# Attention probabilities turned through VectorE and DRAM instead of TensorE, in a two-layer graph attention kernel

## The chip, the cores and the metric

The kernel runs on one core of one Trainium2 chip, in fp32 throughout. The metric is device time in microseconds for one execution. A profiled execution gives the traces that are read below.

## The reference

The input x has 128 groups of 64 nodes with 768 features, and adj is a 64 x 64 mask per group. Two residual graph layers follow each other. Layer 0, which the change touches, has 12 heads of 64 features:

```python
h = jnp.einsum('bnd,ade->bane', feat_in, W)
th = jnp.tanh(h)
attn = th @ w_src + swapaxes(th @ w_dst)          # per head, 64 x 64
attn = jnp.where(attn >= 0, attn, 0.2 * attn)
attn = jnp.where(~adj, -999.0, attn)
attn = jax.nn.softmax(attn, axis=-1)
feat_out = elu(jnp.einsum('banm,bame->bane', attn, h) + b)
gate = jax.nn.sigmoid(feat_in @ H_w.T + H_b)
return gate * feat_out + (1.0 - gate) * feat_in
```

x plus this result is normalised over its features. Layer 1 is an attention with 6 heads of 128 features over the same groups of 64, masked by adj, with products by Wq, Wk, Wv and Wf, and again a sum with x and a normalisation. The change leaves it as it is; only the values of layer 1 (product by Wv) are made while layer 0 runs.

## The kernel before

Rows of x (group and node) are cut into 64 tiles of 128 rows, two groups to a tile, and two tiles make a pair: 32 pairs. Layer 0 takes the first half of the run, one pair after another. For each pair p there are fifteen "a" products (a scheme that saves multiplications, over the 768 x 1536 matrix of W and H_w; class `Fifteen`, L944) and seven "v" products (`Job`, L345) that make the values of layer 1 for earlier pairs. The table `TURN` writes out by hand in which order these 22 products of a pair follow each other on TensorE; "u" is a v product of pair p - 2, "v" one of pair p - 1. `EARLY` and `LAST` do the same for the first four pairs and the end.

Everything else of layer 0 is hung onto these products. The tables `NEW`, `OLD` and `SUMS` (with variants for early and last pairs) hold a due time for each small step, in units of products. `NEW` counts from the products that the step needs, `OLD` from the begin of the pair that follows the step's own pair. The loop over `items` (at the end of layer 0) issues one product, then all steps due at that place, in order of their due times. Each engine runs its instructions strictly in the order of issue. All transfers of layer 0 are issued by the SP queue, in order too: when one transfer has to wait, those behind it wait with it. Three buffers matter below: `pT` (one), `work` tiles (five) and the PSUM banks "m" (two).

For a tile t the steps around the change are these:

- `products` (L984 to L986) takes the tanh of h and multiplies it by the two weight rows; `terms` (L994 to L999) sums per head and turns the sums by a VectorE stream transpose, which turns each block of 32 x 32 by itself; `send` (L1003) stores them in DRAM and `fetch` (L1008) loads them back, broadcast to all rows of their group, as `dd`.
- `logits` and `more_logits` (L1037, ScalarE, 12 instructions) add the two terms with the leaky slope; `masked` (L1051, L1057, VectorE) puts in the mask and takes the row maxima.
- `exps` (L1066, ScalarE, 12 instructions) takes the exponentials into `prob`: rows are nodes n, columns are (head, node m).
- `probs_by_nodes` (L1081) turns `prob` so that m is on the partitions: six TensorE transposes of 128 x 128 into PSUM and two ScalarE copies into `pT`, both in the helper `transposed` (L1078, L1079). The same helper turns x1 later, in `by_features`.
- `other_half` (L1024, L1025) loads `hx`, the half of h that lies on the other group's partitions.
- `attend` (L1099) multiplies: for each of six columns j, two halves of the heads a and two groups g, a matmul with a 64 x 64 block of `pT` as its weights and 65 columns of h or `hx` as its moving operand (the 65th is ones and gives the denominator of the softmax). That makes 24 matmuls per tile.
- `features` (L1115, L1116, L1123) and `elu1`, `gated`, `stats`, `power`, `normed`, `by_features`, `spill_rows` go on to the tile's normalised rows, and `v_begins` starts the sums for the v products.

For the odd tile of a pair (`probs1`, `attend1`) the place of attention is behind the sixth product of the next pair's `TURN`, for the even one (`probs0`, `attend0`) behind the eleventh.

Of the kernel before, what the change touches and what calls it, by code (L numbers as in the profile page):

```python
# [9 lines left out]
F32 = mybir.dt.float32  # L10
# [5 lines left out]
P = 128  # L16
N = 64
# [4 lines left out]
HALF = D // 2  # L22
H0, E0 = 12, 64
J0 = H0 // 2
# [106 lines left out]
]  # L131
TURN = "u6 a1 u5 a0 u7 a5 a3 u3 a8 u4 a6 a7 a9 a10 a2 a12 a4 a14 a11 v1 a13 v2".split()

EARLY = (
    "a0 a5 a3 a8 a6 a1 a7 a10 a9 a2 a12 a4 a11 a14 a13".split(),
# [9 lines left out]
SUMS = dict(next6=0.2, next9=0.4, next2=4.5, next3=6.2, next0=7.2, next5=10, next8=5.3, own10=3.7, own12=7.2,  # L145
    own13=2.7)
OLD = dict(probs1=3.8, gtanh1=0, resid1=3.6, attend1=5.3, feat1=5.5, elu1=7.2, gated1=7.4, stats1=7.5, pow1=9,
    norm1=10.1, byf1=11.3, spill1=13.9, logits0=2.3, leaky0=3.1, masked0=4, exps0=5, gtanh0=5.6,
    resid0=7.2, probs0=8, attend0=10.5, feat0=10.8, elu0=12.5, gated0=12.6, stats0=15, pow0=15.2,
    norm0=16.1, byf0=17.2, spill0=22.3, sum0=15.6, sum1=18, sum2=22, sum3=27, spillT=22, spillV=12.8,  # L150
    mask=8.9, adj=4.5, xT=1.4, inputs1=10.3, inputs0=17.5, plus1=16.3, plus0=19.2)
NEW_LAST = dict(tanh1=2, terms1=4, bias1=6.4, send1=4.7, hx1=10.9, fetch1=9.3, logits1=9.6, leaky1=10.4,
    masked1=11, exps1=12.5, tanh0=1.8, terms0=5, bias0=5, send0=6.2, hx0=4.9, fetch0=8.3, gbias0=10.8,
    gbias1=2.2)
SUMS_LAST = dict(next6=0.4, next9=6.4, next2=0.6, next3=5, next0=15.7, next5=0.1, next8=11.3, own10=1.2, own12=7.8,
    own13=10.6)
OLD_LAST = dict(probs1=2.1, gtanh1=0.8, resid1=5.8, attend1=5, feat1=5.5, elu1=7, gated1=7.4, stats1=9.3,
    pow1=10.8, norm1=11.6, byf1=13.3, spill1=14.5, logits0=3, leaky0=3.4, masked0=4.4, exps0=5,
    gtanh0=8, resid0=9.7, probs0=8.8, attend0=10.5, feat0=11.8, elu0=12.4, gated0=12.8, stats0=14.5,
    pow0=14.6, norm0=15.6, byf0=16.5, spill0=22.4, sum0=16.5, sum1=17.2, sum2=18.5, sum3=24.4,  # L160
    spillT=24.8, spillV=11, mask=5.1, adj=-1.3, xT=3.4, inputs1=5.9, inputs0=18.5, plus1=13.6,
    plus0=18.9)
OLD_EARLY = [
    dict(probs1=1.8, gtanh1=-2, resid1=0, attend1=3.5, feat1=5, elu1=6, gated1=6.1, stats1=7, pow1=8,
        norm1=9, byf1=10, spill1=12.3, logits0=3.5, leaky0=4.3, masked0=5.2, exps0=6.2, gtanh0=3.5,
        resid0=4.8, probs0=8.3, attend0=11, feat0=12, elu0=12.2, gated0=13.1, stats0=14.5, pow0=15,
        norm0=15.2, byf0=17.5, spill0=18, sum0=10.2, sum1=18, sum2=19.3, sum3=26.7, spillT=18.4,
        spillV=11.2, mask=6, adj=3.7, xT=0, inputs1=10.2, inputs0=17.3, plus1=12.2, plus0=18.8),
    dict(probs1=-4.1, gtanh1=1.3, resid1=2.5, attend1=3, feat1=4.7, elu1=5.1, gated1=5.8, stats1=6.8,
        pow1=7, norm1=8, byf1=10.3, spill1=10.7, logits0=3, leaky0=4, masked0=5, exps0=6.3, gtanh0=2.7,  # L170
        resid0=6.8, probs0=8.3, attend0=9.7, feat0=10.5, elu0=12, gated0=12.4, stats0=13, pow0=14,
        norm0=16, byf0=17, spill0=21.7, sum0=11.7, sum1=18, sum2=19.5, sum3=24.7, spillT=22.2,
        spillV=15.2, mask=9, adj=5.2, xT=-3.5, inputs1=8.2, inputs0=11.7, plus1=17, plus0=15.2),
    dict(probs1=1, gtanh1=1.6, resid1=4.3, attend1=3.5, feat1=4, elu1=4.2, gated1=5.4, stats1=7.7,
        pow1=8.5, norm1=10.5, byf1=11.3, spill1=13.2, logits0=2.8, leaky0=3.8, masked0=5, exps0=7.3,
        gtanh0=-1.3, resid0=6.6, probs0=8.3, attend0=9.5, feat0=11.5, elu0=12, gated0=12.1, stats0=13.3,
        pow0=13.5, norm0=14, byf0=16.3, spill0=18, sum0=16.5, sum1=18.2, sum2=16, sum3=21, spillT=16.8,
        spillV=8, mask=5, adj=-4.8, xT=2.9, inputs1=10.2, inputs0=13.5, plus1=11.7, plus0=17),
    dict(probs1=1.8, gtanh1=1.3, resid1=1.8, attend1=3.5, feat1=4.5, elu1=6, gated1=6.4, stats1=7.4,
        pow1=8, norm1=9, byf1=11.5, spill1=14.8, logits0=2.7, leaky0=4.3, masked0=4.5, exps0=5.9,  # L180
        gtanh0=-0.8, resid0=7.7, probs0=8, attend0=9, feat0=10.5, elu0=11.2, gated0=12.1, stats0=14,
        pow0=15, norm0=16, byf0=17.2, spill0=18.3, sum0=14.8, sum1=18.5, sum2=22, sum3=20, spillT=21.1,
        spillV=11.6, mask=8.7, adj=2, xT=-0.2, inputs1=13.5, inputs0=16, plus1=13.6, plus0=19.7),
]
# [27 lines left out]
def kernel(  # L212
# [611 lines left out]
    with ExitStack() as ph, ExitStack() as ph_r:  # L824
# [69 lines left out]
        def work(name):  # L894
            return sb.tile([P, D], F32, tag="work", name=name, bufs=5)
# [164 lines left out]
        def exps(t):  # L1060

            att, mx = st[t].pop("att"), st[t].pop("mx")
            prob = work(f"prob_{t}")
            for a in range(H0):
                at = 2 * (a % J0) + a // J0
                S.activation(  # L1066
                    prob[:, at * N : (at + 1) * N],
                    att[:, a * N : (a + 1) * N],
                    AF.Exp,
                    bias=mx[:, a : a + 1],  # L1070
                )
            st[t]["prob"] = prob

        def transposed(dst, src, name):

            b = bank("m", name)
            for c in range(3):
                T.transpose(b[:, c * P : (c + 1) * P], src[:, c * P : (c + 1) * P], ident)  # L1078
# [12 lines left out]

        def attend(t):
            pT, h, hx = st[t].pop("pT"), h_of(t), st[t].pop("hx")
            av = [bank("m", f"av_{t}_{a}") for a in range(2)]
            for j in range(J0):
                for a in range(2):
                    rows = slice(a * N, (a + 1) * N)
                    for g in range(2):
                        T.matmul(  # L1099
                            av[a][g * N : (g + 1) * N, j * EP : (j + 1) * EP],  # L1100
                            pT[rows, j, g * N : (g + 1) * N],
                            h[rows, a * J0 + j, :] if a == g else hx[rows, j, :],
                            start=True,
                            stop=True,
                        )
            st[t]["av"] = av
# [154 lines left out]
        for p in range(NP + 1):  # L1261
# [15 lines left out]

            if q >= 0:
                for key, f in (
                    ("probs", probs_by_nodes), ("gtanh", gate_tanh), ("resid", residual), ("attend", attend),  # L1280
                    ("feat", features), ("elu", elu1), ("gated", gated), ("stats", stats), ("pow", power),
                    ("norm", normed), ("byf", by_features), ("spill", spill_rows),
                ):
# [246 lines left out]
```

## Time and profile before

| | |
|---|---|
| median of the runs | 2811.52 us (2810.82 to 2812.22, 2 runs) |
| the profiled execution's own time | 2813.49 us |
| its span, from the first to the last instruction | 2811.7 us |
| mean granted TensorE clock | 0.997 |
| TensorE busy / VectorE / ScalarE / GpSimd | 99% / 66% / 48% / 52% of the span |
| layer 0 | about the first 1450 us |
| one pair of layer 0 (644.0 to 688.4 us) | TensorE 44.4 us busy, VectorE 33.4, ScalarE 30.3, GpSimd 26.6 |
| transposes of prob (L1078, pTp) | 384, mean 276 ns, 55.4 us busy |
| their copies (L1079, pT) | 128, median 478 ns |
| attention matmuls (L1099, av) | 3072 instructions on TensorE, two for each matmul |
| DMA | 198038 packets, 325.52 MB |

The profile names engines PE (TensorE matmuls), PEld (TensorE weight loads), DVE (VectorE), ACT (ScalarE), POOL (GpSimd) and SP. A line of a group or of a timeline gives the source line, engine, operation, what is written <- what is read, and shapes. Times in a timeline count from the start of the span. A line of stretches gives, for each engine, its busy time with the number of instructions in brackets, then the granted TensorE clock, the DMA share and the GB/s. Matmuls are pipelined: the duration of one is longer than its distance to the next, so the work of TensorE is read from start to start. The rows of transfers give the number, the size of each and the median time from issue to landing.

### The profile page before, as it was taken

How to read it: one execution, taken by the hardware profiler on the slowest of the kernel's cores; microseconds unless marked ns; L12 is line 12 of the kernel's file. 1: busy time of each engine (PE TensorE's matmuls, PEld its weight loads, DVE VectorE, ACT ScalarE, POOL GpSimd, SP SyncE). 2: the span in 40 equal slices, each digit the busy share in tenths (PEclk: the TensorE clock that was granted, in tenths of full speed). 3: DMA queues.
4: the chain of work that ended last, by engine and by line, in shares of the span. 5: the costliest groups of instructions: out<-in, count | busy, mean ns of one | idle time of the engine just before them, and what ended most of it. 6: DMA issues, size and time to landing. Idle time of an engine off the chain costs nothing.

```text
span 2811.7 us, 47352 instructions
## 1 busy us (share of the span) xinstructions
PE 2776.4 (99%) x17472; PEld 1931.9 (69%) x17472; DVE 1851.2 (66%) x3215; ACT 1357.1 (48%) x3434; POOL 1453.7 (52%) x1501
## 2 busy tenths in 40 slices
PE   7999999999999999999999999999999999999998
PEld 3455555555555555555568888888888888888887
DVE  7867877777777777867764555555555555554557
ACT  4666676766767666676753222333222333221333
POOL 5556556565655656555454345445345435345435
PEclk9999999999999999999999999999999999999999
DMA  5354444544545445333444112222212222212212
GB/s 186 110 167 155 137 159 133 173 151 143 167 138 165 147 148 166 110 125 104 170 163 161 63 52 88 91 83 80 69 48 86 91 84 80 72 50 81 91 61 83
DMA packets 198038, 325.52 MB, mean 116 GB/s; under 512 B 46896, under 2 KB 125744, under 8 KB 197808
## 3 DMA queue, kind: packets, MB, share of 16 engines
q1 hardware_dynamic: 197520, 322.10, 34.8%
q8 instruction: 139, 2.28, 0.3%
q14 instruction: 91, 0.75, 0.1%
q10 hardware_dynamic: 288, 0.39, 0.0%
HBM read 198.48 MB, written 111.15 MB: 110 GB/s over the span
## 4 chain that ended last, share of the span: by engine, by line
PE 95%; DVE 1%; ACT 0%; issue 0%; DMA 0%; POOL 0%; ACTq 0%; DVEq 0%
PE y_a L944 18%; PE z_a L944 9%; PE z_q L524 9%; PE z_k L524 9%; PE y_v L345 9%; PE z_o L571 9%; PE y_k L524 6%; PE y_q L524 6%; PE y_o L571 6%; PE z_v L345 4%; PE x_v L345 2%; PE av L1099 2%; PE cp L689 2%; PE sp L629 2%; PE pTp L1078 2%; PE x1Tp L1078 1%
## 5 line engine op out<-in xcount | busy, mean ns | idle before, releaser
L944 PE MATMUL y_a<-wa,sx 128*128 128x512 f32 x1024 | 487.3, 605 | 19.2 <-DVE sx L882 7.9
L944 PEld LDWEIGHTS y_a<-wa,sx 128*128 128x128 f32 x1024 | 189.3, 192 | 221.6 <-issue 173.4
L488 POOL TENSOR_TENSOR so<-ctxT 128x256 f32<-128x256 f32 x224 | 157.7, 728 | 287.8 <-ACT ctxT L716 286.9
L716 ACT ACTIVATE ctxT<-cp,bv_c 128x256 f32<-128x256 f32 x192 | 73.8, 486 | 451.1 <-PE cp L689 451.1
L1129 POOL TENSOR_TENSOR x<-hg,x 128x768 f32<-128x768 f32 x64 | 111.8, 1748 | 211.1 <-ACT hg L1203 211.1
L524 PE MATMUL z_q<-xs,wa 128*128 128x256 f32 x896 | 211.9, 380 | 0.0
L655 ACT ACTIVATE sc<-sc 128x512 f32<-128x512 f32 x45 | 28.4, 630 | 379.7 <-DVE sc L652 379.7
L571 PE MATMUL z_o<-wf,so 128*128 128x256 f32 x896 | 209.3, 382 | 2.4 <-DVE y L584 2.4
L1037 ACT ACTIVATE att<-dd,sd 128x64 f32<-128x64 f32 x768 | 190.4, 336 | 33.4 <-DMA dd<-dstd 33.4
L986 POOL TENSOR_TENSOR th<-th,wsd 128x768 f32<-128x768 f32 x64 | 117.1, 1829 | 167.5 <-DVE th L985 167.5
L1066 ACT ACTIVATE prob<-att,mx 128x64 f32<-128x64 f32 x768 | 190.3, 335 | 25.8 <-DVE mx L1057 24.5
L524 PE MATMUL z_k<-xs,wa 128*128 128x256 f32 x840 | 198.5, 380 | 0.0
L397 POOL TENSOR_TENSOR rs_b<-ve_b,minus_half 128x1 f32<-128x1 f32 x64 | 40.9, 638 | 302.5 <-DVE ve_b L395 289.5
L584 DVE TENSOR_TENSOR y<-y,z_o 128x256 f32<-128x256 f32 x320 | 128.6, 419 | 100.3 <-PE z_o L571 100.2
L1051 DVE COPY_PREDICATED_SCALAR att<-nadj,neg 128x768 f32 x64 | 69.2, 1081 | 182.7 <-ACT att L1037 182.6
L571 PEld LDWEIGHTS z_o<-wf,so 128*128 128x128 f32 x896 | 169.1, 190 | 26.5 <-POOL so L488 2.6
L524 PEld LDWEIGHTS z_q<-xs,wa 128*128 128x128 f32 x896 | 170.2, 190 | 22.7
L944 PE MATMUL z_a<-wa,xT 128*128 128x512 f32 x384 | 183.1, 600 | 0.0
L524 PEld LDWEIGHTS z_k<-xs,wa 128*128 128x128 f32 x840 | 160.0, 190 | 21.3
L960 DVE TENSOR_TENSOR hg<-hg,y_a 128x512 f32<-128x512 f32 x225 | 151.9, 676 | 24.2 <-PE y_a L944 18.7
L760 POOL TENSOR_TENSOR y<-y,bf_bc 128x768 f32<-128x768 f32 x64 | 114.6, 1813 | 96.8 <-issue 56.0
L488 POOL TENSOR_TENSOR xs<-r,r 128x512 f32<-128x512 f32 x112 | 146.7, 1328 | 23.7 <-PE y_k L524 12.4
(154 smaller groups left out, 6427.1 us busy)
## 6 DMA issues: line engine op xcount, KB each, us to landing
xT<-in_xT_dram SPq DMA_DIRECT2D x32, 768.0 KB, 6.9
x<-in_x_dram SPq DMA_DIRECT2D x64, 384.0 KB, 3.4
dd<-dstd SPq DMA_DIRECT2D x128, 192.0 KB, 3.4
x1d<-x SPq DMA_DIRECT2D x64, 384.0 KB, 4.9
x1Td<-x1T SPq DMA_DIRECT2D x32, 768.0 KB, 4.8
vd<-v SPq DMA_DIRECT2D x64, 384.0 KB, 3.0
r<-x1Td SPq DMA_DIRECT2D x96, 256.0 KB, 3.2
v<-vd SPq DMA_DIRECT2D x192, 128.0 KB, 3.0
```

The lines of the kernel that those rows point to most:

```text
L345: T.matmul(to[:, : self.n], lhsT, rhs, start=kc == 0 and not more, stop=kc == HK - 1, skip_group_check=more,)
L488: G.tensor_tensor(t, self.of(x[0]), self.of(x[2]), x[1])
L524: T.matmul(b[:, half * W2 : (half + 1) * W2], w[:, kc, half * P : (half + 1) * P], x[:, kc, :], start=half == kc == 0 and not more, stop=k ...
L571: T.matmul(b[:, :W2], x[:, kc, :], w[:, kc, :], start=kc == 0 and not more, stop=kc == 1, skip_group_check=more,)
L584: V.tensor_tensor(at, at, self.banks[path][:, :W2], ALU.add if sign > 0 else ALU.subtract)
L760: G.tensor_tensor(y, y, pools["bf"], ALU.add)
L944: T.matmul(b, x[:, kc, :], wa[:, n, kc, :], start=kc == 0 and not more, stop=kc == 1, skip_group_check=more,)
L960: V.tensor_tensor(at, at, b, ALU.add if sign > 0 else ALU.subtract)
L986: G.tensor_tensor(th[:, 1, :], th[:, 1, :], wsd[:, 1, :], ALU.mult)
L1037: S.activation(att3[:, a], dd3[:, a], AF.Prelu, bias=sd[:, H0 + a : H0 + a + 1], alpha=LEAKY)
L1066: S.activation(prob[:, at * N : (at + 1) * N], att[:, a * N : (a + 1) * N], AF.Exp, bias=mx[:, a : a + 1],)
L1129: G.tensor_tensor(xp, gate_of(t), xp, ALU.mult)
```

## The change

`probs_by_nodes` becomes one VectorE stream transpose of the whole tile and a store to DRAM. A new step `probs_back` loads the tile back with four transfers, one for each block of 32 partitions, and so does the part of the turn that crosses blocks of 32. `exps` writes `prob` in another order of columns (half of the group's nodes first, then head), so that one stream transpose covers it; the transpose writes each partition with the head index innermost, so that the rows of the store are runs of 192 floats. `attend` picks its weights from the new layout with a step of six floats. `back1` and `back0` are the due times of the new step, and the other due times are set anew; in `TURN` two products change places.

```diff
-TURN = "u6 a1 u5 a0 u7 a5 a3 u3 a8 u4 a6 a7 a9 a10 a2 a12 a4 a14 a11 v1 a13 v2".split()
+TURN = "u6 a1 u5 u7 a0 a5 a3 u3 a8 u4 a6 a7 a9 a10 a2 a12 a4 a14 a11 v1 a13 v2".split()
...
-NEW = dict(tanh1=1.7, terms1=5.5, bias1=5.7, send1=7.2, hx1=11.6, fetch1=7.7, logits1=9, leaky1=9.2,
-    masked1=10.3, exps1=12.7, tanh0=1.5, terms0=3, bias0=7.7, send0=4.2, hx0=8.6, fetch0=4.3,
-    gbias0=5.8, gbias1=1.5)
+NEW = dict(tanh1=3.4, terms1=5.7, bias1=5.9, send1=6.4, hx1=14.4, fetch1=7, logits1=10.2, leaky1=10.6,
+    masked1=11.3, exps1=12.5, tanh0=1.2, terms0=2.6, bias0=7.7, send0=2.7, hx0=10.9, fetch0=4.5,
+    gbias0=5, gbias1=1.3)
...
-OLD = dict(probs1=3.8, gtanh1=0, resid1=3.6, attend1=5.3, feat1=5.5, elu1=7.2, gated1=7.4, stats1=7.5, pow1=9,
...
-    resid0=7.2, probs0=8, attend0=10.5, feat0=10.8, elu0=12.5, gated0=12.6, stats0=15, pow0=15.2,
...
-    mask=8.9, adj=4.5, xT=1.4, inputs1=10.3, inputs0=17.5, plus1=16.3, plus0=19.2)
+OLD = dict(probs1=2, gtanh1=0, resid1=2.8, attend1=6.4, feat1=6.9, elu1=7.3, gated1=7.5, stats1=8.2, pow1=8.9,
...
+    resid0=8.5, probs0=6.2, attend0=10.5, feat0=10.8, elu0=13, gated0=13.2, stats0=15.2, pow0=15.7,
...
+    spillV=14.3, mask=10.9, adj=5.7, xT=1.2, inputs1=11.5, inputs0=17.8, plus1=16.7, plus0=18.6,
+    back1=4.1, back0=7.8)
...
+    turned_d = [dram.tile([4, P, 32 * J0], F32, name=f"turnedd_{t}") for t in range(2 * NP)]
...
             prob = work(f"prob_{t}")
+            by_head = prob.rearrange("p (a h j m) -> p a j h m", a=2, h=2, m=32)
             for a in range(H0):
-                at = 2 * (a % J0) + a // J0
                 S.activation(
-                    prob[:, at * N : (at + 1) * N],
-                    att[:, a * N : (a + 1) * N],
+                    by_head[:, a // J0, a % J0],
+                    att[:, a * N : (a + 1) * N].rearrange("p (h m) -> p h m", h=2),
                     AF.Exp,
                     bias=mx[:, a : a + 1],
                 )
...
         def probs_by_nodes(t):
             prob = st[t].pop("prob")
-            pT = sb.tile([P, J0, P], F32, tag="pT", name=f"pT_{t}", bufs=1)
-            for half in range(2):
-                transposed(
-                    pT[:, 3 * half : 3 * half + 3, :],
-                    prob[:, half * HALF : (half + 1) * HALF],
-                    f"pTp_{t}_{half}",
+            turned = work(f"turned_{t}")
+            V.transpose(
+                turned.rearrange("p (b t j) -> p b j t", b=4, j=J0), prob.rearrange("p (b j t) -> p b j t", b=4, j=J0)
+            )
+            nc.sync.dma_start(out=turned_d[t].rearrange("b p c -> p b c"), in_=turned.rearrange("p (b c) -> p b c", b=4))
+
+        def probs_back(t):
+            pT = sb.tile([P, 4, 32 * J0], F32, tag="pT", name=f"pT_{t}", bufs=1)
+            for b in range(4):
+                nc.sync.dma_start(
+                    out=pT[32 * b : 32 * b + 32], in_=turned_d[t][b].rearrange("(r m) c -> m r c", m=32)
                 )
             st[t]["pT"] = pT
...
                         T.matmul(
                             av[a][g * N : (g + 1) * N, j * EP : (j + 1) * EP],
-                            pT[rows, j, g * N : (g + 1) * N],
+                            pT[rows, 2 * g : 2 * g + 2].rearrange("p r (t j) -> p j (r t)", j=J0)[:, j],
                             h[rows, a * J0 + j, :] if a == g else hx[rows, j, :],
```

The step `probs_back` stands between `probs_by_nodes` and `gate_tanh` in the list of steps. `SUMS` and the tables for early and last pairs are set anew in the same way. On the SP queue the order around the odd tile becomes: the two fetches of the even tile's terms, xT, the store of the turned tile, the odd tile's two hx loads (before, these stood ahead of xT), then the four loads; for the even tile: adj, two hx loads, the store, the four loads. A load of x rows for the pair now stands ahead of the odd tile's fetch.

More of the change, by code (lines that the diff above doesn't have):

```diff
@@ L140 @@
 EARLY_OLD = (19, 38, 57)
[L142 to L151 removed]
+NEW = dict(tanh1=3.4, terms1=5.7, bias1=5.9, send1=6.4, hx1=14.4, fetch1=7, logits1=10.2, leaky1=10.6,
+    masked1=11.3, exps1=12.5, tanh0=1.2, terms0=2.6, bias0=7.7, send0=2.7, hx0=10.9, fetch0=4.5,
+    gbias0=5, gbias1=1.3)
+SUMS = dict(next6=2, next9=2.3, next2=5, next3=5.1, next0=5.9, next5=9.7, next8=6.3, own10=1.8, own12=5,
+    own13=1)
+OLD = dict(probs1=2, gtanh1=0, resid1=2.8, attend1=6.4, feat1=6.9, elu1=7.3, gated1=7.5, stats1=8.2, pow1=8.9,
+    norm1=9.3, byf1=11, spill1=17, logits0=2.8, leaky0=3.1, masked0=3.3, exps0=5.2, gtanh0=5.9,
+    resid0=8.5, probs0=6.2, attend0=10.5, feat0=10.8, elu0=13, gated0=13.2, stats0=15.2, pow0=15.7,
+    norm0=16.4, byf0=17.5, spill0=20, sum0=14.6, sum1=18, sum2=22.8, sum3=26.5, spillT=18.5,
+    spillV=14.3, mask=10.9, adj=5.7, xT=1.2, inputs1=11.5, inputs0=17.8, plus1=16.7, plus0=18.6,
+    back1=4.1, back0=7.8)
 NEW_LAST = dict(tanh1=2, terms1=4, bias1=6.4, send1=4.7, hx1=10.9, fetch1=9.3, logits1=9.6, leaky1=10.4,
[L153 removed]
+    masked1=11, exps1=12.5, tanh0=1.8, terms0=5, bias0=5, send0=6.2, hx0=5.1, fetch0=8.3, gbias0=10.8,
     gbias1=2.2)
@@ L156 @@
     own13=10.6)
[L157 to L160, printed above, removed]
+OLD_LAST = dict(probs1=2.5, gtanh1=0.8, resid1=5.8, attend1=5.6, feat1=5.7, elu1=7, gated1=7.4, stats1=9.3,
+    pow1=10.8, norm1=11.6, byf1=13.3, spill1=14.5, logits0=3.4, leaky0=3.5, masked0=4.4, exps0=5,
+    gtanh0=8, resid0=9.7, probs0=7.3, attend0=10.9, feat0=12.2, elu0=12.72, gated0=13.12, stats0=14.74,
+    pow0=14.94, norm0=15.76, byf0=16.58, spill0=22.48, sum0=16.5, sum1=17.2, sum2=18.5, sum3=24.4,
@@ L161 @@
     spillT=24.8, spillV=11, mask=5.1, adj=-1.3, xT=3.4, inputs1=5.9, inputs0=18.5, plus1=13.6,
-    plus0=18.9)
+    plus0=18.9, back1=3.8, back0=8.9)
 OLD_EARLY = [
[L164 to L168, printed above, removed]
@@ L169 @@
-    dict(probs1=-4.1, gtanh1=1.3, resid1=2.5, attend1=3, feat1=4.7, elu1=5.1, gated1=5.8, stats1=6.8,
-        pow1=7, norm1=8, byf1=10.3, spill1=10.7, logits0=3, leaky0=4, masked0=5, exps0=6.3, gtanh0=2.7,
-        resid0=6.8, probs0=8.3, attend0=9.7, feat0=10.5, elu0=12, gated0=12.4, stats0=13, pow0=14,
-        norm0=16, byf0=17, spill0=21.7, sum0=11.7, sum1=18, sum2=19.5, sum3=24.7, spillT=22.2,
-        spillV=15.2, mask=9, adj=5.2, xT=-3.5, inputs1=8.2, inputs0=11.7, plus1=17, plus0=15.2),
@@ L174 @@
[L174 to L183, printed above, removed]
+    dict(probs1=0.8, gtanh1=-2, resid1=0, attend1=4.4, feat1=5.9, elu1=6.72, gated1=6.92, stats1=7.54,
+        pow1=8.45, norm1=9.36, byf1=10.18, spill1=12.48, logits0=3.5, leaky0=4.3, masked0=5.2,
+        exps0=6.2, gtanh0=3.5, resid0=4.8, probs0=7, attend0=11, feat0=12, elu0=12.2, gated0=13.1,
+        stats0=14.5, pow0=15, norm0=15.2, byf0=17.5, spill0=18, sum0=10.2, sum1=18, sum2=19.3,
+        sum3=26.7, spillT=18.4, spillV=11.2, mask=6, adj=3.7, xT=0, inputs1=10.2, inputs0=17.3,
+        plus1=12.2, plus0=18.8, back1=2.4, back0=8.6),
@@ new lines @@
+    dict(probs1=-5.1, gtanh1=1.3, resid1=2.5, attend1=3, feat1=4.7, elu1=5.1, gated1=5.8, stats1=6.8,
+        pow1=7, norm1=8, byf1=10.3, spill1=10.7, logits0=3, leaky0=4, masked0=5, exps0=6.3, gtanh0=2.7,
+        resid0=6.8, probs0=7.1, attend0=10.7, feat0=11.5, elu0=12.8, gated0=13.2, stats0=13.6,
+        pow0=14.5, norm0=16.4, byf0=17.2, spill0=21.9, sum0=11.7, sum1=18, sum2=19.5, sum3=24.7,
+        spillT=22.2, spillV=15.2, mask=9, adj=5.2, xT=-3.5, inputs1=8.2, inputs0=11.7, plus1=17,
+        plus0=15.2, back1=-3.5, back0=8.7),
@@ new lines @@
+    dict(probs1=0, gtanh1=1.6, resid1=4.3, attend1=3.6, feat1=4.1, elu1=4.3, gated1=5.48, stats1=7.76,
+        pow1=8.55, norm1=10.54, byf1=11.32, spill1=13.22, logits0=2.8, leaky0=3.8, masked0=5, exps0=7.3,
+        gtanh0=-1.3, resid0=6.6, probs0=8.1, attend0=11.7, feat0=13.7, elu0=13.9, gated0=14.1,
+        stats0=14.62, pow0=14.82, norm0=15.02, byf0=16.74, spill0=18.44, sum0=16.5, sum1=18.2, sum2=16,
+        sum3=21, spillT=16.8, spillV=8, mask=5, adj=-4.8, xT=2.9, inputs1=10.2, inputs0=13.5,
+        plus1=11.7, plus0=17, back1=1.6, back0=9.7),
@@ new lines @@
+    dict(probs1=0.8, gtanh1=1.3, resid1=1.8, attend1=4.4, feat1=5.4, elu1=6.72, gated1=7.12,
+        stats1=7.94, pow1=8.45, norm1=9.36, byf1=11.68, spill1=14.98, logits0=2.7, leaky0=4.3,
+        masked0=4.5, exps0=5.9, gtanh0=-0.8, resid0=7.7, probs0=6.7, attend0=10.3, feat0=11.8,
+        elu0=12.24, gated0=13.14, stats0=14.78, pow0=15.65, norm0=16.52, byf0=17.46, spill0=18.56,
+        sum0=14.8, sum1=18.5, sum2=22, sum3=20, spillT=21.1, spillV=11.6, mask=8.7, adj=2, xT=-0.2,
+        inputs1=13.5, inputs0=16, plus1=13.6, plus0=19.7, back1=2.4, back0=8.3),
@@ L1279 @@
                 for key, f in (
-                    ("probs", probs_by_nodes), ("gtanh", gate_tanh), ("resid", residual), ("attend", attend),
+                    ("probs", probs_by_nodes), ("back", probs_back), ("gtanh", gate_tanh), ("resid", residual), ("attend", attend),
                     ("feat", features), ("elu", elu1), ("gated", gated), ("stats", stats), ("pow", power),
```

## The prediction

> **What bounds the kernel now.** I read the page's busy shares and chain first, then TensorE's busy time by stretches, then its waits, then the timelines of one pair.
>
> ```profile
> PE 2776.4 (99%) x17472; PEld 1931.9 (69%) x17472; DVE 1851.2 (66%) x3215; ACT 1357.1 (48%) x3434; POOL 1453.7 (52%) x1501
> ...
> PE 95%; DVE 1%; ACT 0%; issue 0%; DMA 0%; POOL 0%; ACTq 0%; DVEq 0%
> ...
> 644.00:688.40 44.40, 44.40 (x224) 23.38 (x223) 33.41 (x52) 30.30 (x81) 26.56 (x28) 1.00 0.47 147
> ```
>
> The last line is one pair of tiles in layer 0, columns as PE, PEld, DVE, ACT, POOL, clock, DMA share. TensorE is busy all of its 44.4 us; VectorE has 11 us to spare, ScalarE 14. The list of TensorE's waits between 200 and 1400 us is empty: in steady layer 0 nothing ever makes it wait. So layer 0 is a TensorE stream of fixed length, and two things count: what leaves the stream, and whether a new wait enters it.
>
> **What leaves the stream.** Busy time overstates a transpose, because a matmul's modelled tail overlaps the next. I take start to start, from TensorE's timeline around an attention tile:
>
> ```profile
> 1026.52 2.10 PE L345 MATMUL z_v<-wv,sv_v 128*128 128x384 f32 x6
> 1028.45 1.88 PE L944 MATMUL y_a<-wa,sx 128*128 128x512 f32 x4
> 1030.17 0.82 PE L1078 MATMUL pTp<-ident,prob 128*128 128x128 f32 x6
> 1030.83 2.10 PE L345 MATMUL y_v<-wv,sv_v 128*128 128x384 f32 x6
> 1032.76 1.88 PE L944 MATMUL z_a<-wa,sx 128*128 128x512 f32 x4
> ...
> 1034.57 0.27 PE L1099 MATMUL av<-hg,pT 64*64 64x65 f32 x1
> ```
>
> Six transposes take 1030.83 - 1030.17 = 0.66 us of the stream (the busy sum of 55.4 us for 384 would give 0.87). 64 tiles x 0.66 = **-42 us**. The same lines price the work around: a "v" product 1.93 us, an "a" product 1.72, the attention matmuls 0.95 with their edges. The 128 ScalarE copies of 0.48 us also go; ScalarE isn't the bound, so that is worth nothing.
>
> **What is added, at no cost of its own.** One VectorE stream transpose per tile. The nearest row is layer 1's, 0.70 us for 512 elements a partition, so 768 cost 1.05 us: 2.1 us per pair out of 11 spare. Exponentials written as two runs of 32 instead of one of 64: the rows of the prelu (L1037, written as 2 x 32) and of the exponentials take 336 and 335 ns, so nothing. DMA: 64 tiles x 1024 runs of 768 B, 50 MB. By bytes (322 MB took 34.8% of the span) that is +5.4% of the span, or 11 points of layer 0; by packets (197520) twice that. 0.47 becomes 0.58 to 0.69, no bound. SP issues five more transfers per tile, 0.4 us each; it mostly waits. The other entries of the tables shift small steps among their neighbours on engines with the spare time above; apart from two transfers named below I count them as nothing, and half a microsecond later in a chain would cost what a late chain costs below, 30 x 0.5.
>
> **What is added on the path: a latency.** The matmuls of attention stand in TensorE's fixed order and now need: transpose, store, four loads. I count for the odd tile of a pair, from e, the end of its exponentials.
>
> ```profile
> 1026.41 2.97 ACT L1066 ACTIVATE prob<-att,mx 128x64 f32<-128x64 f32 x12
> ...
> 1034.92 2.97 ACT L1066 ACTIVATE prob<-att,mx 128x64 f32<-128x64 f32 x12 [0.60 <-DVE mx L1057]
> ```
>
> So e = 1029.38, 2.86 after the start of product u5 (1026.52); the even tile's end is 8.51 later. Before e nothing moves much: the chain to it runs from the fetched terms (ScalarE waited for that fetch 30 times) and stands at the same products in both plans. One load of x (384 KB) now goes ahead of the odd tile's fetch; that can add up to its own transfer, under 1 us. I take 0 and keep 1 for the range.
>
> Room: the new order is u5, u7, a0, a5, a3, attention: 2 x 1.93 + 3 x 1.72 = 9.0 us from the start of u5, less 2.86 = **6.2 us** after e (5.2 before, 1034.57 - 1029.38).
>
> Need, from the DMA rows:
>
> ```profile
> x1d<-x SPq DMA_DIRECT2D x64, 384.0 KB, 4.9
> ...
> vd<-v SPq DMA_DIRECT2D x64, 384.0 KB, 3.0
> v<-vd SPq DMA_DIRECT2D x192, 128.0 KB, 3.0
> ...
> hx<-hg SPq DMA_DIRECT2D x128, 97.5 KB, 5.0
> ```
>
> Transpose done at e+1.1. Store of 384 KB: the v rows' 3.0 (fastest of its tile 2.0; the x rows' 4.9 stand behind another store, this one behind nothing but the end of an xT load): e+4.2. While it flies SP issues the two hx loads that are moved behind it (0.5 and 0.6 us), and in some pairs a piece of weight sums; that fits. SP then stands at the first load, which waits for the store; behind it are only adj, the even tile's hx, weight sums and x rows, none needed soon. Four loads in a row: nearest is layer 1's four loads of v, 0.43 us each to issue and 3.0 to land, so the last lands at e+4.2+1.3+3.0 = **e+8.5**. hx, issued by e+2.7 with 5.0 to landing, is there at e+7.1: late as well, but hidden under the loads.
>
> TensorE therefore waits 8.5 - 6.2 = 2.3 us (ends: 0.8 with every transfer at its fastest, 5 with the store at 4.9 and the fetch late). Even tile: need e+8.5+8.5 = e+17.0; its attention comes at 6.2 + 2.3 + 0.95 + (u3, a8, u4, a6 = 7.3) = e+16.8, so 0.2 more. What is late next: everything on TensorE, by the same amount, so the following pair's chain keeps its distance and the wait returns in each pair. About 30 of 32 pairs: 30 x 2.5 = **+75 us**.
>
> **The clock.** Does a wait cost more than its length? Rows of before, same columns as above:
>
> ```profile
> 72.75:76.16 3.41, 1.46 (x4) 0.49 (x3) 3.34 (x8) 0.00 (x0) 1.62 (x3) 1.00 0.38 115
> 76.16:79.58 3.42, 3.42 (x7) 1.40 (x6) 1.65 (x3) 1.03 (x1) 2.64 (x2) 0.50 0.93 323
> ...
> 174.00:178.00 4.00, 3.76 (x15) 2.11 (x14) 1.54 (x3) 2.92 (x9) 3.10 (x2) 1.00 0.11 45
> ```
>
> A wait of 1.95 us (for POOL's sx, at 73.9) lies in the first stretch, and in the next the clock is 0.50 for 3.42 us; behind a wait of 1.43 us at 172.2 it stays 1.00. The Trainium skill ("TensorE: Matmul & The Clock Gate", section What's actually happening) has the clock fall after at least one whole idle window of about 3.4 us, windows running freely. By the page waits of 2.5 us are harmless, +0; by the row a wait of about 1.9 us inside one window is enough, and a dip costs 3.42 / 2 = 1.7 us. A 2.3 us wait falls far enough into one window about half of the time: 15 x 1.7 = 26 us. I follow the row but, since waits scatter about 2.3, count ten dips: **+17 us**.
>
> **Stepped reads.** The transpose now writes, and the attention weights are loaded, with a step of 6 floats, 24 bytes; no row of before has that. The Trainium skill ("Advanced Engine Details and Errata", section SBUF Cachelines) speaks against the change: SBUF has 16-byte lines, and an access pattern that touches each line once pays. If weight loads took twice as long and were all that holds the attention matmuls back, their 0.85 us would double: +0.85 x 64 = 54 us; the transpose at 2.1 us would lengthen each chain by 1.05, 31 us. If the loads stay behind the matmuls, 0. The nearest rows, all unstepped, don't decide; I take 0 and keep up to 85 for the range.
>
> **Sum:** 2811.7 - 42 + 75 + 17 = 2862, rounded to 2860. That sum is against the profiled span (2811.7, its own time 2813.5); the median of the runs shown is 2811.5, so it stands for those as well.
>
> **Rivals.**
> - *The chain fits* (the transfer is hidden anyway): store 2.0, loads 1.0 + 2.0, so ready at e+6.1, no wait, and the 42 us are kept: 2770. For it: fastest landings of 2.0 do occur, and the order of products was moved to give 1 us more room. Against: it needs the fastest in nearly every pair.
> - *Slower, by the clock*: the wait is about 3 us, so that every pair trips it: -42 + 30 x 3 + 30 x 1.7 = +99, 2911. It decides from a wait of some 1.95 us in one piece. For it: the row at 76 us. Stepped weight loads would land in the same place: 2860 + 54 = 2914.
> - *VectorE becomes the bound*: 33.4 + 2.1 (4.2 if stepped) of 44 us per pair; no.
>
> **Chances.** Chain fits 0.18 (2755 to 2800); waits with few dips 0.48 (2810 to 2890, centre 2860); waits with the clock or stepped loads 0.34 (2880 to 2960). 80% range: 2770 to 2925. Two per cent (56 us, about what a measurement of this kernel can tell from no change) means below 2755 or above 2868. Below: only if the early waits went too, 0.03. Above: all but a little of the third case and a quarter of the second, 0.45. Within: 0.52.
>
> **What would show it.** In the profile after: no pTp rows, TensorE's matmuls down by 384; a new wait of its weight loads at the attention line for pT, over 2 us, once per pair at the odd tile, seldom at the even one; the odd tile's exponentials still ending 2.9 us after the start of u5; store near 3.0, loads 3.0 to landing; clock dips to 0.50 in layer 0; attention matmuls still 0.85 us per tile; the stepped transpose near 1.05. The prediction is wrong if pT lands within 6.2 us of e, if waits of over 2 us leave the clock at 1.00, or if the attention matmuls stretch.

## The result, and the profile after

The changed kernel takes 2976.03 us (2974.34 to 2977.71, 2 runs) against 2811.52 us: 5.9% slower, ratio 1.0585 (95% interval 1.0540 to 1.0631). The forecast was 2860, at most 2925. Its sign holds, its size doesn't: 164.5 us were lost where 49 were expected.

The page of the changed kernel, busy shares and the shares of the chain of waits (they answer to the first fence of the prediction):

```profile
PE 2842.6 (96%) x17088; PEld 1965.6 (66%) x17088; DVE 1911.8 (64%) x3279; ACT 1309.8 (44%) x3306; POOL 1448.0 (49%) x1501
...
PE 45%; DVE 1%; DMA 0%; ACT 0%; issue 0%; SPq 0%; ACTq 0%; POOL 0%; DVEq 0%; POOLq 0%
```

TensorE has 384 matmuls fewer and yet 66 us more busy time; the chain can no longer be followed on TensorE through layer 0 (45% where it was 95%). Next, its stretches: one pair, and two stretches of 3.41 us inside it (columns as in the prediction: length, PE, PEld, DVE, ACT, POOL, granted clock, DMA share, GB/s).

```profile
709.54:712.95 3.41, 2.45 (x50) 2.17 (x51) 1.79 (x4) 3.38 (x10) 0.14 (x1) 1.00 0.73 183
712.95:716.36 3.41, 3.41 (x7) 1.86 (x6) 2.34 (x5) 1.68 (x3) 1.53 (x1) 0.50 0.52 177
692.00:739.77 47.77, 46.18 (x211) 24.42 (x210) 35.51 (x53) 28.24 (x75) 25.99 (x28) 0.96 0.55 171
```

A pair takes 47.77 us instead of 44.2. TensorE idles for 1.6 us of it, and behind that idle time it runs a whole stretch at half its clock. TensorE's waits between 200 and 1400 us, where there were none before (us in total, times, longest):

```profile
PE av L1110 <- DMA pT<-turnedd: 43.2, 49, 4.2
PE y_a L950 <- ACT hg L970: 9.0, 11, 1.2
```

The timeline of that pair around its odd tile's attention (start, us, engine, line):

```profile
699.64 2.97 ACT L1072 ACTIVATE prob<-att,mx 128x64 f32<-128x64 f32 x12
699.73 2.10 PE L351 MATMUL z_v<-wv,sv_v 128*128 128x384 f32 x6
...
702.65 1.59 DVE L1090 STREAM_TRANSPOSE turned<-prob 128x768 f32<-128x768 f32 x1 [1.74 <-ACT prob L1072]
...
704.27 0.38 SPq L1093 DMA_DIRECT2D turnedd<-turned  x1
...
706.92 1.77 SPq L1098 DMA_DIRECT2D pT<-turnedd  x4
707.03 1.88 PE L950 MATMUL y_a<-wa,sx 128*128 128x512 f32 x4
...
710.15 0.29 PE L1110 MATMUL av<-hg,pT 64*64 64x65 f32 x1 [1.24 <-DMA pT<-turnedd]
...
710.94 0.29 PE L1110 MATMUL av<-hx,pT 64*64 64x65 f32 x1 [0.35 <-DMA pT<-turnedd]
...
712.46 3.76 PE L351 MATMUL z_v<-wv,sv_v 128*128 128x384 f32 x6
```

Here e, the end of the exponentials, is 699.64 + 2.97 = 702.61, 2.88 after product u5 began (forecast 2.86). The transpose ends at e+1.6 (1.1), the loads start at e+4.3 (4.2), and over all pairs the last of them lands at a median of e+8.1 (8.5). TensorE would have been free for attention at a median of e+6.3 (6.2). So the latency chain is as forecast; what TensorE does with it is not: attention starts as soon as the first block is there, then stops again for the next ones, and takes from 710.15 to 712.46, 2.31 us where it took 0.86. The part of it that is no wait shows in the rows of attention's weight loads and matmuls (shortest, median, longest in ns), first before, then after:

```profile
L1099 PEld LDWEIGHTS av<-hg,pT x1536: 128/135/137, 60.7 to 1445.9; 64*64 64x64 f32 x192
L1099 PE MATMUL av<-hg,pT x1536: 215/218/269, 60.7 to 1446.0; 64*64 64x65 f32 x192
```

```profile
L1110 PEld LDWEIGHTS av<-hg,pT x1536: 183/205/217, 63.0 to 1608.6; 64*64 64x64 f32 x192
L1110 PE MATMUL av<-hg,pT x1536: 272/274/380, 63.0 to 1608.7; 64*64 64x65 f32 x192
```

The group of the transpose (busy us, mean ns, then VectorE's idle time before it):

```profile
L1090 DVE STREAM_TRANSPOSE turned<-prob 128x768 f32<-128x768 f32 x64 | 102.3, 1599 | 110.6 <-ACT prob L1072 110.6
```

The DMA rows of the round trip (KB each, median us from issue to landing; forecast 3.0 and 3.0):

```profile
turnedd<-turned SPq DMA_DIRECT2D x64, 384.0 KB, 2.9
pT<-turnedd SPq DMA_DIRECT2D x256, 96.0 KB, 2.3
```

In the trace's clock rows TensorE stands at half clock for 131.7 us in 30 dips (20.6 us in 3 before); 19 of the 30 begin between 200 and 1400 us. Half of that time is lost: 66 against 10 us, 56 more.

Where along the run the time goes is read from the starts of the "a" products, which both kernels have in the same number: the changed kernel is behind by 31 us after the first four pairs, then by 3.6 us more in the median steady pair (47.77 against 44.15, pairs 6 to 30), and by 12 more in the last pair, with the rest behind it.

### The profile page after: what moved, and what is told of

It reads as the page before. It is cut to its first block, busy times and chain, and to the rows that moved or that the text cites. A ratio compares the mean times of both kernels' runs of the same rounds, so it can differ in the third digit from the quotient of the medians.

```text
span 2975.9 us, 47147 instructions
## 1 busy us (share of the span) xinstructions
PE 2842.6 (96%) x17088; PEld 1965.6 (66%) x17088; DVE 1911.8 (64%) x3279; ACT 1309.8 (44%) x3306; POOL 1448.0 (49%) x1501
## 5 line engine op out<-in xcount | busy, mean ns | idle before, releaser
L992 POOL TENSOR_TENSOR th<-th,wsd 128x768 f32<-128x768 f32 x64 | 124.4, 1944 | 204.1 <-DVE th L991 204.1
L1177 ACT ACTIVATE x<-x,sh_a,rs_a 128x768 f32<-128x768 f32 x64 | 65.8, 1027 | 247.3 <-DVE sh_a L1176 247.3
L1090 DVE STREAM_TRANSPOSE turned<-prob 128x768 f32<-128x768 f32 x64 | 102.3, 1599 | 110.6 <-ACT prob L1072 110.6
L1110 PEld LDWEIGHTS av<-hg,pT 64*64 64x64 f32 x1536 | 105.0, 204 | 99.6 <-issue 59.3
L1110 PE MATMUL av<-hg,pT 64*64 64x65 f32 x1536 | 119.5, 285 | 51.7 <-DMA pT<-turnedd 51.4
```

What stands on the lines that cost most here:

```text
L992: G.tensor_tensor(th[:, 1, :], th[:, 1, :], wsd[:, 1, :], ALU.mult)
L1090: V.transpose(turned.rearrange("p (b t j) -> p b j t", b=4, j=J0), prob.rearrange("p (b j t) -> p b j t", b=4, j=J0))
L1110: T.matmul(av[a][g * N : (g + 1) * N, j * EP : (j + 1) * EP], pT[rows, 2 * g : 2 * g + 2].rearrange("p r (t j) -> p j (r t)", j=J0)[:, j], ...
```

## The experiments

Theory when they began: three things add up, the stepped reads (taken as 0 in the forecast), the wait for `pT`, and clock dips, which the two make together. Rivals: the waits and dips alone; the retimed steps of the tables. The times of each are set against runs of the kernel before on the same chip (2811.65 to 2813.94 us).

### The stepped weights alone

The kernel before, with `pT` laid out head innermost, so that its weights are read (and its two copies written) with the 24-byte step. Nothing else changes.

```diff
-pT = sb.tile([P, J0, P], ...)
+pT = sb.tile([P, P, J0], ...)
-pT[rows, j, g * N : (g + 1) * N],
+pT[rows, g * N : (g + 1) * N, j],
```

> The kernel before, with one thing of the change: the attention weights lie with the head index innermost, so that each weight load reads with a step of 24 bytes (ScalarE's copies out of PSUM write them so). No round trip, no new order. If stepped weight loads are what stretches the attention matmuls (from 0.71 to 1.32 us per tile from the first to the last start), they stretch here by the same 0.6 us per tile: 64 x 0.6 = +39 us, about 2851 us, no new waits, clock 0.997. If the stretch comes only from blocks of pT that land one after another, the attention matmuls stay at 0.71 us and the time at 2812 us. The copies may take longer than 0.48 us; ScalarE has 14 us of 44 to spare per pair, so that shows only in its own rows.

Measured: 2855.57 us, +41.6, ratio 1.0151 (1.0136 to 1.0166); clock 0.998, no new waits. One line of that tile's rows:

```profile
L1099 PEld LDWEIGHTS av<-hg,pT x1536: 183/205/214, 59.8 to 1488.3; 64*64 64x64 f32 x192
```

These are the changed kernel's durations without its round trip. Attention takes 1.53 us per tile instead of 0.86, start to start; 64 x 0.67 = 43, the whole loss. The ScalarE copies that write with the step went from 478 to 881 ns, and that sum leaves no cost to them. So the step is a cost of its own.

### The change without the step

The changed kernel with the plain order of elements in the transpose. A weight load takes one run of columns here, so each 64-column load becomes two of 32: 48 matmuls per tile for 24.

```diff
-turned.rearrange("p (b t j) -> p b j t", b=4, j=J0), prob...
+turned.rearrange("p (b j t) -> p b j t", b=4, j=J0), prob...
-for g in range(2):
+for r in range(4):
-    pT[rows, 2 * g : 2 * g + 2].rearrange("p r (t j) -> p j (r t)", j=J0)[:, j],
+    pT[rows, r, j * 32 : (j + 1) * 32],
```

> The changed kernel with nothing stepped: the stream transpose writes in plain order, and each attention matmul of 64 weight columns becomes two of 32 columns, which are contiguous. Stepped loads as a cause of their own: attention back to 0.7 to 0.8 us per tile (39 us less), the stream transpose from 1.59 to about 1.05 us, so pT lands 0.5 us earlier and the wait per pair falls from about 2 to 1.5 us (17 us less), and fewer dips of the clock: 2976 - 39 - 17 - up to 40 = 2880 to 2920. If stepping is not the cause: 2976 within 10 us.

Measured: 2910.36 us, +96.4, ratio 1.0346 (1.0331 to 1.0362). Two groups (busy us, mean ns):

```profile
L1111 PEld LDWEIGHTS av<-hg,pT 64*32 64x32 f32 x3072 | 68.0, 108 | 86.3 <-issue 40.1 <-PE y_a L950 28.5 <-DMA pT<-turnedd 12.8
...
L1090 DVE STREAM_TRANSPOSE turned<-prob 128x768 f32<-128x768 f32 x64 | 62.6, 978 | 107.4 <-ACT prob L1072 107.4
```

Taking the step away saves 68 us, more than putting it into the kernel before cost. Plain attention with 48 matmuls takes 1.11 us (still 0.25 more than before), so 64 x 0.42 = 27 us are direct. The rest is the clock: 12 dips of 57 us in all for 30 of 131.7, 37 us less lost. Between 200 and 1400 us TensorE waits 43.2 us for `pT` with the step and 36.2 without, a like sum, but it comes with 19 dips in the one kernel and 2 in the other: the step makes dips out of waits that alone mostly leave the clock up. The share of the stepped transpose alone, which makes each chain 0.6 us longer, was not measured.

### Taking the wait away

Attention is given old data: the loads fetch the tile two before. In the first form the loads stay behind the store in the SP queue; in the second they also stand ahead of it; the third is the second without the step.

```diff
-in_=turned_d[t][b]...                          (all three)
+in_=turned_d[t - 2 if t > 5 else t][b]...
-store(t), then four loads                      (second and third)
+four loads, then store(t)
```

> The changed kernel, but the four loads fetch the turned tile of the pair before (from tile 6 on), so that they need not wait for this tile's store; every instruction stays, the attention weights are one pair old. If the round trip's latency is the main cost, the waits of attention for pT (81 us) and with them most of the 29 dips of the clock (56 us) go: 2976 - 81 - 50 = about 2845. If the clock dips for another reason (the stretched attention matmuls keep TensorE less busy), the dips stay: about 2895. If the retimed tables are the main cost: above 2920.

> The changed kernel; from tile 6 on the four loads fetch the tile of the pair before (attention weights one pair old), and each store is issued behind those loads, so that SP no longer stands at a store while the loads are due. All instructions stay. The previous try left the loads behind a blocked store, and attention still waited 52 us for pT. If the waits for pT and the dips that follow them are the larger half: waits for pT below 15 us, dips only in the first 200 us and at the end, pair period from 47.7 to 44.15 - 1.3 + 1.2 = about 44.1 us, the whole about 2976 - 26 x 3.6 - 10 = 2870. If the dips come from the stretched attention matmuls, the period stays at 45.7 or more: 2915.

> The same, with nothing stepped as well (32-column attention weights, plain stream transpose): what is left when waits and steps are both taken out. The two causes together explain the steady part: pair period 44.15 - 1.32 + 2 x 0.25 = 43.3 us, 2870 - 26 x 0.8 = about 2850, hardly a dip, the rest over 2812 lying in the first four and the last two pairs. If something else in the new order costs time, the period stays above 44.1.

Measured: the first 2944.26 us (ratio 1.0470, 1.0452 to 1.0487), the second 2911.84 (1.0356, 1.0341 to 1.0372), the third 2887.61 (1.0272, 1.0255 to 1.0289). The first missed and was no test: SP waited at the store for the transpose, with the loads behind it, and TensorE still waited 52.1 us for `pT`. In the second, the waits for `pT` from tile 6 on are nearly gone (between 200 and 1400 us 1.9 us, 2 times, for 43.2), and others come in their place:

```profile
PE x1Tp L1084 <- ACT x L1185: 13.9, 27, 0.6
PE y_a L950 <- ACT hg L970: 11.7, 10, 1.8
```

So taking away the wait for `pT`, with its dips (30 to 10), brings 64 us with the step and 20 without (96.4 - 76.0). With the step that is less than what went (waits for `pT` in the whole run 69.4 to 19.8 us, half of the dips 66 to 23), since other waits take the place. And 100 us of the loss stay with hardly a wait of the steady pairs for `pT`. Waits and dips alone are not the story.

### Later attention

The version without the step, with attention and what follows from it one product later, to give the chain its room.

```diff
-attend1=6.4, feat1=6.9, ... attend0=10.5, feat0=10.8, ... sum1=18, spillT=18.5
+attend1=7.4, feat1=7.9, ... attend0=11.5, feat0=11.8, ... sum1=19, spillT=19.5
```

> A kernel with the right data: nothing stepped, and in the table for steady pairs attention of both tiles and the steps behind it stand one product later. The room behind e grows from 6.2 to 8.1 us, the need falls from 8.1 to 7.6. If the wait is just need minus room, it goes: pair period 43.3 us, 2908 - 26 x 2.3 = about 2850. If the wait moves along (the later steps make the next pair's chain later too), the period stays at 45.7: 2908.

Measured: 2973.64 us (1.0577, 1.0562 to 1.0593). A miss: the waits for `pT` fell from 60.2 to 27.1 us, but products now wait for h (VectorE, 42.5 us, 56 times) and transposes for x1 (40.5 us, 29 times). The room for attention is taken from the steps behind it, and these had none to give.

### The new order and due times with the old transposes

TensorE's transposes in the changed order and due times (`probs0` at 8).

```diff
-V.transpose(turned, prob); store; four loads
+transposed(pT[:, 3 * half : 3 * half + 3, :], prob[...], ...)     # as before
```

> The changed kernel's order of products and due times with the six TensorE transposes and ScalarE copies of before in place of the stream transpose, the store and the loads (the even tile's transposes put at 8, behind the odd tile's attention, since there is one pT). What the retimed tables cost by themselves. The round trip as the cause: 2812 within 15 us, hardly a wait on TensorE. The tables as the cause: at least 40 us more than before, 2850 or above, with waits for hg rows.

Measured: 2882.16 us (1.0247, 1.0230 to 1.0264). Too impure to count: with `probs1` at 2 the transposes stood ahead of the end of their exponentials and waited 17.5 us for `prob`. A cleaner form follows below.

### The round trip in the old order

The opposite: order and due times of before, with the round trip (no step) only in tiles 8 to 59. First with old data, then with each tile's own; then for even tiles only, attention one product later; then all of them with the odd tile's attention 1.7 products later as well.

```diff
+def by_trip(t): return 8 <= t < 60             # third: and t % 2 == 0
-attend0=10.5, feat0=10.8, elu0=12.5, ...       # third and fourth
+attend0=11.5, feat0=11.8, elu0=13.4, ...
-attend1=5.3, feat1=5.5, elu1=7.2, ...          # fourth
+attend1=7, feat1=7.3, elu1=8.6, ...
```

> The kernel before with its own order and due times. Only tiles 8 to 59 are turned by the stream transpose (plain read and write) and the round trip; from tile 10 on the four loads fetch the data of the tile two before and stand ahead of the store, so attention waits for nothing (its values are not the reference's). Theory A (the six transposes are worth their 0.66 us per tile, and the losses left over in the kernels without a wait, about 1.9 us per pair, come from the retimed tables): per tile -0.66 + 0.25 (48 matmuls with plain weights in place of 24), 52 tiles, -21: about 2790. Theory B (the round trip itself disturbs the stream, by its transfers, its place in the SP queue or its VectorE time): 2812 or more.

> The same, but with each tile's own data: store, then four loads, right behind the transpose, in the order and due times of the kernel before. Room at the odd tile is 5.2 us after the end of its exponentials; the plain chain needs 8.1 - 0.6 = 7.5. If the room decides: a wait of about 2.3 us in each of 26 pairs, 60 us, and a clock dip in most of them (1.7 us each, up to 44): 2790 + 60 + 20 to 44 = 2870 to 2895. If the retimed tables of the changed kernel are what costs, about 2850 or less.

> Only the even tiles from 8 to 58 take the round trip (plain), the odd ones keep their TensorE transposes; attention of the even tile stands one product later, the five steps behind it up to one product later. Room for the even tile: 5.2 + 0.95 + 9.0 - 8.5 + 1.7 = 8.4 us, against 7.5. If a round trip that fits is worth its transposes: 26 x (0.66 - 0.25) = -11, about 2801, faster than the kernel before by 0.4%. If the later steps make TensorE wait for h or x1, 2812 to 2850.

> All tiles 8 to 59 take the round trip (plain), the even tile as in the run for even tiles only, the odd tile's attention 1.7 products later (room 5.2 + 3.0 = 8.2, against 7.5) with its next steps 0.5 to 1.7 later. If room is all that is needed: 2790. If a later attention makes later things late (products that wait for h or for the turned x1): one or more waits of 0.5 to 1.5 us per pair, 2805 to 2850.

Measured: 2970.41 (1.0568, 1.0554 to 1.0583), 3214.49 (1.1432, 1.1417 to 1.1448), 3132.41 (1.1140, 1.1124 to 1.1155) and 3091.44 us (1.0983, 1.0959 to 1.1007). All four missed by far. The first, whose loads wait for no data of their own tile, shows one reason; its SP queue and TensorE at one odd tile:

```profile
690.02 0.54 SPq L841 DMA_DIRECT2D xT<-in_xT_dram  x1
...
691.16 0.47 SPq L1030 DMA_DIRECT2D hx<-hg  x1
691.68 0.68 SPq L1031 DMA_DIRECT2D hx<-hg  x1
692.39 2.52 SPq L1117 DMA_DIRECT2D pT<-turnedd  x4
```

```profile
700.15 0.32 PE L1133 MATMUL av<-hg,pT 64*32 64x65 f32 x2 [4.75 <-DMA pT<-turnedd]
```

The loads are issued 7.8 us ahead of their use and still come late. In the trace's landings xT (768 KB, issued at 690.0) ends at 698.5, and the seven transfers issued behind it end after it, in order, 0.2 to 0.6 us apart, the last piece of `pT` at 700.6. In the old order these small loads stand behind a transfer of 768 KB. That bears on a question that the diff leaves open, why so many due times were changed: in tiles 8 to 59 and without the step, the round trip costs 402 us in the old order and 48 in the new one (below). Which of the retimed entries keep its way free was not taken apart. In the even-tile run VectorE, in order, stood 6.63 us at the reciprocal of late attention, with the sums of h behind it, and products waited 85.2 us (28 times) for h.

### Which part of the run

The changed order, no step, but the first four and last two pairs keep TensorE's transposes and their due times of before (tiles 8 to 59 by the round trip); the same with old data; and the same order with no round trip at all, the transposes behind the end of their exponentials.

```diff
+def by_trip(t): return 8 <= t < 60             # third: none
-OLD_EARLY, OLD_LAST of the change
+OLD_EARLY, OLD_LAST of before
-probs1=2, ... probs0=6.2                       # third
+probs1=4, ... probs0=8
```

> The changed kernel with the plain transpose and plain weights, but only tiles 8 to 59 take the round trip; the first four and the last two pairs keep TensorE's transposes with their due times of before (the steady pairs keep the changed order and due times). The plain version lost 35 us in pairs 0 to 5 and about 21 behind pair 30. If these losses belong to the round trip and the due times of those pairs: 2910 - 35 - 15 = about 2860. If they come from elsewhere (the start-up, or the steady pairs that begin at pair 4): about 2900.

> The same, with loads of the tile two before and stores behind the loads from tile 10 on, so that attention of the middle pairs doesn't wait for its own data (values not the reference's). What is left above the kernel before is the price of the retimed steps in the middle pairs: the version without waits on all tiles showed 1.3 us per pair, so 2811.5 + 26 x 1.3 = about 2845 if it stays, about 2795 (26 x (0.82 - 0.25 - ...) near zero cost and the transposes' gain) if that loss was an echo of the early pairs.

> TensorE's transposes in every tile, with the changed order and due times in the steady pairs only; the transposes stand two items later than in the earlier run with the changed tables (behind the end of the exponentials), early and last pairs have the due times of before. No round trip is left. If the retimed steps cost nothing by themselves, as the forecast took: 2812 to 2818. If they make TensorE wait for h or x1 (1.0 to 1.5 us per pair): 2838 to 2852.

Measured: 2859.24 (1.0166, 1.0149 to 1.0183), 2849.86 (1.0134, 1.0119 to 1.0149) and 2844.87 us (1.0116, 1.0101 to 1.0131), all three close to what was expected. TensorE's longest waits in total, in the version for the middle pairs, the same with old data, and the one without a round trip:

```profile
PE av L1135 <- DMA pT<-turnedd: 33.6, 52, 1.8
```

```profile
PE x1Tp L1095 <- ACT x L1210: 19.0, 29, 0.9
```

```profile
PE y_a L941 <- ACT hg L961: 15.4, 15, 2.3
```

Six pairs at the ends hold 49 us of the loss (96.4 - 47.6). Half of it is waits for `pT`: in the version without the step, 7.9 us in the first 212 us and 16.2 behind 1400 us, where the middle version has none; the other half was not divided further. In the middle, the plain round trip costs only 14 more than the transposes (47.6 - 33.2), and 33 us are lost with the new order and due times without any round trip.

The run with old data warns against adding this up: 52 x (0.66 - 0.25) = 21 us of TensorE's work saved and 33.6 us of waits would give 13, near the 14 measured. But with old data the waits for `pT` fall to 2.8 us and the kernel gains only 9 (47.6 - 38.2), because TensorE now waits 19.0 us for x1 (1.7 with own data). With 21 us less to do and hardly a wait for `pT`, it takes 5 us more than the kernel with the transposes, no difference beyond the noise. In this order, then, work taken from TensorE did not become time; steps behind attention come too late as well. The timeline of the last kernel at one of its waits:

```profile
326.98 2.98 ACT L1034 ACTIVATE att<-dd,sd 128x64 f32<-128x64 f32 x12 [0.80 <-DMA dd<-dstd]
...
329.86 0.46 ACT L972 COPY v<-y_v 128x384 f32<-128x384 f32 x1
...
330.21 0.84 ACT L1076 COPY pT<-pTp 128x384 f32<-128x384 f32 x2
330.95 0.60 ACT L961 ACTIVATE hg<-y_a 128x512 f32<-128x512 f32 x1
...
331.60 1.12 PE L941 MATMUL y_a<-wa,sx 128*128 128x512 f32 x2 [0.97 <-ACT hg L961]
```

ScalarE works through the twelve prelu instructions late, because their terms (`dd`) came late; the read-out of h stands behind them and behind the transposes' two copies into `pT`, and TensorE needs its bank. The changed kernel has no such copies, so the 33 us need not be the exact price of the due times beside the round trip.

### What made the terms late

The changed due times moved two transfers into the chain of the terms on the SP queue: the load of x goes behind the store of the odd tile's terms, and the store of x1 goes between the even tile's store and fetch. Moved back one after the other; the first also in the middle-pairs kernel and in the changed kernel.

```diff
-inputs0=17.8
+inputs0=17.2        # all four
-spill0=20
+spill0=22.3         # last
```

> The kernel with TensorE's transposes and the changed due times in the steady pairs, with one transfer moved back: the load of the even tile's x stands ahead of the store of the odd tile's terms in the SP queue, as before, and not behind it (inputs0 17.2 for 17.8). If the retimed steps cost 33 us because ScalarE waits for this load (1.6 us in 23 of the steady pairs) and reads h out of PSUM late behind it: that wait goes, and 33 shrinks to 5 to 15: 2817 to 2827. If other due times are to blame: 2838 to 2848.

> The same one transfer moved back in the kernel with the plain round trip in the middle pairs only (2859). If the wait for x is what the retimed steps cost there too: 2830 to 2842. If TensorE's wait for pT absorbs it: within 5 us of 2859.

> The changed kernel as it is, with only this load moved back. If it starts the late chain there as well: 20 to 30 us less, 2946 to 2956. If TensorE's wait for pT hides what the load makes late: within 8 us of 2976.

> The last kernel with TensorE's transposes and the changed due times in the steady pairs (2843.6), with a second transfer moved back: the store of the even tile's x1 (384 KB) stands behind the fetch of its terms in the SP queue, as before, and not between the store of the terms and their fetch (spill0 22.3 for 20). In the traces this fetch lands 7.2 us after the store of the terms instead of 5.7, and up to 10.4 instead of 6.5; ScalarE's prelu, and behind it the read-out of h that TensorE waits for, are late by it. If that is the cause: the fetch lands at about 5.7 and 29 us shrink to under 12: 2815 to 2825. If not: 2838 to 2846, and it stays open which due times cost.

Measured: 2843.55 (1.0108, 1.0093 to 1.0123), 2864.46 (1.0177, 1.0162 to 1.0192), 2990.01 (1.0626, 1.0608 to 1.0644) and 2837.45 us (1.0093, 1.0076 to 1.0110). The load of x explains little: between 290 and 1350 us ScalarE's wait for it fell from 37.0 us (23 times) to 7.8 (4 times), and the kernel gained 3, which is within the noise. Beside the round trip moving it back is worth nothing, in the changed kernel it costs 13 (38 dips for 30). With both moved back, the even tile's second fetch lands 6.3 us after the store (median; 7.3 with the change's due times, 5.7 before), and the loss is 24.8 instead of 33.2. So these two account for some 8 of the 33 us. The other 25 stay open: which of the remaining due times holds them was not found.

## Why the prediction was wrong

The four differences below lead from the changed kernel to the kernel before, each a step between two kernels that ran (each against before on its own chip), and sum to the whole. Taken in another order the differences would have other sizes, since the costs act on each other:

| step | us |
|---|---|
| 24-byte step in transpose and weights (changed kernel to the one without the step) | 164.5 - 96.4 = 68 |
| round trip and due times in the first four and last two pairs | 96.4 - 47.6 = 49 |
| round trip for transposes in the steady pairs | 47.6 - 33.2 = 14 |
| new order and due times of the steady pairs | 33 |

**Transposes, -42: not seen as time gained.** The 384 matmuls are gone, and the 0.66 us per tile stands as TensorE's work. But the middle pairs without the wait, with 21 us less work, should have been 21 us below the kernel with the transposes and were 5 above it: other waits took the room.

**Latency and room: right, in part by luck.** e, the room of 6.2 us and the chain (8.1 for 8.5) hold to half a microsecond; the even tile waits for next to nothing, as forecast. But the transpose took 0.5 us longer than counted, and the four loads took that much less. Per pair the wait is 1.0 us ahead of attention and 1.0 inside it, 2.1 with the even tile's, for 2.5.

**"The nearest rows, all unstepped, don't decide; I take 0": this failed most.** Measured alone it is +42 us, in the changed kernel 68. The end was set well ("up to 85", 54 of it weight loads), the value below it was not; and 85 on top of 2860 is 2945, while the range ended at 2925. The Trainium skill ("Advanced Engine Details and Errata", section SBUF Cachelines) was the better guide: it warns of accesses that touch each 16-byte line once, and a weight load went from 135 to 205 ns, the transpose from 978 to 1599. That the line of 16 bytes is the reason was not tested: no run has another step.

**Clock, "I count ten dips": too few.** There are 30, and they cost 56 us more than before, where 17 were counted. The rule of the Trainium skill (a dip needs an idle window, "TensorE: Matmul & The Clock Gate", section What's actually happening) would give none behind waits of 1 us; the row of 1.95 us in one piece gave the right kind of answer, but the forecast asked only for the length of the wait. By the traces (last section) what counts is how much of one window TensorE leaves unfilled, and stretched attention leaves it unfilled too. That fits the step and the wait costing more together than apart.

**"The other entries ... I count them as nothing": wrong, +33 in the steady pairs.** The half microsecond was named ("half a microsecond later in a chain would cost ..."), and something of the kind happened: terms 1.6 us later, read-outs of h behind them. That covers 8 of the 33; what holds the rest stays open.

**"About 30 of 32 pairs" alike: wrong.** The first four and last two pairs lost 49 us without the step, some 8 each, not 2.5; in the changed kernel one wait for `pT` near the end is 8.5 us long.

So both parts of the rival at 2911 to 2914 came true, the dips (though with waits of 2 us and not 3) and the stepped loads, and with them two terms that no case had. The range ended where one of the slower cases did and not where both did.

## What to carry to other kernels

When work leaves the bounding engine for a chain of other engines and transfers, price first how the bounding engine will read the layout that the chain leaves behind: here the step alone cost 42 us, as much as the removed work was counted for. Then treat each shift in a packed schedule as a cost until a row shows its slack, and ask for every transfer what stands ahead of it on its queue. Costs that share a window of the clock gate are not to be added one by one.

## What the runs showed of the hardware

**The clock falls at the end of a fixed window of 3.413 us that was filled too little.** In all 20 traces every dip starts within 0.03 us of a grid of 3.413 us through the first one. I count a window's time as filled by each matmul's full-clock start-to-start time (0.43 us for 512 columns, 0.32 for 384, 0.03 for one of attention) and take the rest as idle, between 200 and 1450 us, outside dips. Behind windows with at least 2.2 us idle a dip followed every time (some 200 windows); from 2.0 to 2.2 in about half of 50; below 2.0 in 1 of some 6700. The count doesn't ask whether the idle time lay in one piece or in several. This is read over traces, not tried by itself.

**The changed kernel locks to that grid.** Its later dips mostly come 47.79 us apart, 14 windows, and its median pair takes 47.77: the wait of the next pair then falls into the same place of a window. That this is what keeps the dips coming is a reading, not tried.

**Transfers of the one SP queue land in order.** In each of the 20 traces, of 620 to 881 such transfers issued between 200 and 1400 us, none landed ahead of one issued before it. The four loads of 96 KB issued behind one of 768 KB in the stretch shown above took 6.2 to 7.4 us (round trip in the old order, old data), where 2.3 is the median in the changed kernel.
